# The last four attention steps of a gated cross-attention and FFN layer, ordered in one list with the FFN work that is left

## The chip, the cores and the metric

The kernel runs on one core of a Trainium2 chip. A core has five engines with their own instruction queues: TensorE (PE, matrix products), VectorE (DVE), ScalarE (ACT), GpSimd (POOL) and SyncE (SP, which here issues every DMA). Each runs its own queue strictly in order, and they wait for one another through semaphores. The metric is the time of one execution on the device in microseconds (us); three runs of the kernel before took 3007.0, 3010.42 and 3010.99 us, a median of 3010.42 us.

## The reference

32 batches of 224 tokens (512 wide) attend to 750 context tokens (384 wide) with 16 heads of 32, then go through an FFN of 2048 whose weights are rounded to -1, 0, 1 and whose activations are rounded to 8 bits per token.

```python
def xattn(x, y, pad_mask, Wq, Wkv):          # per batch, 16 heads
    q = x @ Wq.T; k, v = split(y @ Wkv.T)
    attn = softmax(where(mask, q * d**-0.5 @ k.T, -1e9))
    return attn @ v
x = x + tanh(g_xattn) * xattn(layernorm(x), ctx, mask, Wq, Wkv)
x = x + tanh(g_ffn) * ffn(layernorm(x))
# ffn: bitlinear(gelu(bitlinear(x, w1, b1)), w2, b2)
# bitlinear: act_quant(rmsnorm(x)) @ weight_quant(w).T + b
```

## The kernel before

**Attention.** 128 steps (`steps`, N = 128): 32 batches by four groups of four heads, numbered n = 0 to 127. The loop at line 1006, `for n in range(N - 1)`, writes out the work of step n in six slots. The even slots hold one third of the next step's score products for the maxima (`maxima`, line 312: PE writes tile `sm`, DVE reduces it to `mx`); the odd slots hold one third of this step's products, from which ACT takes the exponential (`weights`, line 369: PE writes `se`, ACT writes `p`, POOL adds `p` into `acc`). `sm` and `se` share one buffer of four PSUM banks (`ps_s`), so PE may write the next `sm` only when ACT has read `se`, and the next `se` only when DVE has reduced `sm`. What PE does meanwhile is whatever stands between them in its queue: products for keys (`pk`), values (`pv`), queries (`pq`), the last step's output (`po`, from `p` and `v`), and FFN products. A step opens with `turn_max`: PE turns the negated maxima (`pn`), ACT copies them to `nT`, and `weights` needs `nT`. `finish` and `store` (lines 436 and 445) scale the output on POOL (`yo`) and write it with four DMAs to a DRAM buffer `o_d`.

**FFN.** 28 pairs of 128-row tiles (`NF` = 28, numbers 0 to 27), each cut by `ffn_units` into units: load and fetch (x and `o_d`), add, stats, rsqrt, norm, max, sa0 to sa2 (scales), grid and round (rounding), turn (a transposing DMA); then for each of the two tiles b0 to b3 (four times four products `ph`, DVE writes `h`), gelu and square on ACT, hm (maxima of `h`), sb0 to sb2 (scales, with a chain of small operations for the inverse root), cgrid, cround, cturn (a transposing DMA `hT<-hq`), c0 and c1 (16 products each into `po`, from `w2q` and `hT`) and out. A pair can begin only when the attention rows that it covers are stored; the last pair needs step 127's columns.

**What sets the order.** Engine queues follow program order. In the loop, `Ffn.fill` (line 857) puts FFN units into each slot, as many as `rooms` allow: PE room is 2.5 or 1.9 less what the slot holds, plus `late` (line 888), which is 0.3 for every row tile that is ready but not done beyond a number: `LATE` (3) up to 24 stored batches, and 3 again after that, which is from step 96 on. What is left after step 126 goes to `drain` (line 893): units of the last step (pair number 28 in its list) and of the FFN pairs left, put in order by a planner with a table of durations (`TAKES_US`, line 777); in each turn it takes, of the units that can begin soonest, the one with the longest chain behind it. A unit that can run on either of two engines gets the one that ends it first. There the waits of the last step are listed in `LAST` (line 800), and no gelu may stand before the last exponential, since the two need different ACT tables. Inside the loop each gelu loads its table, and then loads the exponential's again (`b_gelu`, line 671, with the activation `warm`).

Of the kernel before, what the change touches and what calls it, by code (L numbers as in the profile page):

```python
# [24 lines left out]
def flamingo_gated_layer(  # L25
# [495 lines left out]

    draining = []
# [33 lines left out]
    def ffn_units(i):  # L556
# [6 lines left out]
        def a_load():  # L563
            if i >= NF - 2:
                both = yp.tile([P, NYC * M], F32, tag="y", name=f"xo_{i}")
                both = both[:, : 2 * TG * D].rearrange("p (a t d) -> p a t d", a=2, t=TG)
                s["xg"], s["og"] = both[:, 0], both[:, 1]
            else:
# [6 lines left out]
            if i < NF - 1:  # L575
                a_fetch()

        def a_fetch():
            sp.dma_start(s["og"], o_d[rows, :].rearrange("(t p) d -> p t d", p=P))
# [4 lines left out]
        def a_stats():  # L584
            st = smf.tile([P, TG, 6], F32, tag="st2", name=f"st2_{i}")
            s["mv"] = smf.tile([P, TG, 2], F32, tag="mv2", name=f"mv2_{i}")
            for t in range(TG):
                dve.bn_stats(st[:, t, :], s["xg"][:, t, :])
                dve.bn_aggr(s["mv"][:, t, :], st[:, t, :])

        def a_rsqrt():
# [3 lines left out]
            s["nm"] = smf.tile([P, TG], F32, tag="nm2", name=f"nm2_{i}")  # L595
            small[0].tensor_scalar(s["nm"], s["mv"][:, :, 0], -1.0, None, ALU.mult)
# [107 lines left out]
        def c_round(t):  # L704
            if i < NF - 2:
                s["hq", t] = fp.tile([P, F], BF16, tag="hq", name=f"hq_{i}_{t}")
            else:
                s["hq", t] = xp.tile([P, F], BF16, tag="x", name=f"hq_{i}_{t}")
# [24 lines left out]
        if i == NF - 1:  # L733
            first[1:] = [("fetch", 0, "load", 0, 0, 0, a_fetch), ("add", 0, "fetch", 0, 0, 0, a_add)]
# [3 lines left out]
            ("norm", 2, "rsqrt", 0, 1.2, 0, a_norm),  # L738
# [39 lines left out]
        "load": [[("SP", 2.7)]], "fetch": [[("SP", 4.9)]],  # L778
# [12 lines left out]
        "top": [[("PE", 0.3), ("ACT", 0.4)]],  # L791
        "w": [[("PE", 1.1), ("ACT", 1.7)]],
        "val": [[("PE", 2.9), ("DVE", 0.9)]], "vlast": [[("PE", 4.0), ("DVE", 0.9)]],
        "fin": [[("POOL", 0.6)]], "sto": [[("SP", 3.6)]],
    }

    QUEUE_US = {"sto": 1.9, "turn": 1.9, "cturn": 1.5, "load": 0.5, "fetch": 0.5, "out": 0.4}


    LAST = {  # L800
        name: [(NF, at) for at in after.split()]
        for name, after in {
            "w0": "top", "w1": "w0", "w2": "w1", "val": "", "fin0": "val", "sto0": "fin0",
            "vlast": "w2 val", "fin1": "vlast fin0", "sto1": "fin1 sto0",
        }.items()
    }

    class Ffn:
# [3 lines left out]
        def __init__(self):  # L812
# [3 lines left out]
            self.at = {}  # L816

        def behind(self, pair, name):
# [4 lines left out]
                "fetch": [(NF, "sto1")],  # L823
# [4 lines left out]
            if pair >= NF - 2:  # L828
                before = {"fetch": before["fetch"]}
            if name[-1].isdigit():  # L830
# [9 lines left out]
                    f"gelu{t}": [(NF, "w2")] * len(draining),  # L840
# [3 lines left out]
            if pair == NF:  # L844
                before = LAST
            return [at for at in before.get(name, []) if at[0] >= 0]

        def ready(self, pair, unit):
            name, lag, after = unit[:3]
            lag = lag if not draining else 0  # L850
# [37 lines left out]
        def late(self, stored, more):  # L888

            ready = stored * S // P - TG * self.next + sum(p[1][-1][0][:3] == "out" for p in self.parts)  # L890
            return 0.3 * max(0, ready - (LATE if stored < B - 8 else 3) - more)

        def drain(self, more):
# [3 lines left out]
            draining.append(True)  # L897
            free = {"PE": 0.0, "ACT": 0.0, "DVE": 4.3, "POOL": 5.0, "SP": 0.0}
            end = {}

            def takes(name):
                kind = name.rstrip("0123456789")
                return TAKES_US.get(kind) or TAKES_US[kind + name[-1]]

            self.parts.insert(0, [NF, more])
# [3 lines left out]
            left = {}  # L909

            def rank(at):

                if at not in left:
                    left[at] = 0.0
                    left[at] = sum(us for _, us in takes(at[1])[0]) + max(
                        (rank(x) for x in behind if at in behind[x]), default=0.0
# [3 lines left out]
            behind = {  # L920
                (pair, u[0]): [(pair, u[2] or "")] + self.behind(pair, u[0])
                for pair, units in self.parts for u in units
            }

            def course(at, way):

                t = max(
# [198 lines left out]
```

## Time and profile before

| | |
|---|---|
| runs | 3007.0, 3010.42, 3010.99 us; median 3010.42 us |
| the profiled execution | 3009.68 us, of which its span is 3007.9 us |
| busy over the span | PE 2896.7 us (96%), POOL 2087.6 (69%), DVE 1735.9 (58%), ACT 1409.6 (47%) |
| mean granted TensorE clock | 0.989 |
| `pn` of step 96, 124, 127 begins at | 2204.1, 2837.5, 2902.4 us |
| the last store of attention output is issued at | 2929.43 us |

The span runs from the first to the last instruction; 1.8 us lie around it. The rows of `pn` mark where a step begins. A row of the timeline gives start, duration, engine, operation, what it writes and reads, its shape and how many follow one another; in brackets stand the idle time of the engine before it and what ended that. A fp32 product counts as two MATMULs there.

### The profile page before, as it was taken

To read this page: it belongs to the slowest core of one execution; us is meant where nothing else is said; L and a number is where in the kernel's file an instruction comes from. 1 tells how busy PE (TensorE), PEld (TensorE's weight loads), DVE (VectorE), ACT (ScalarE), POOL (GpSimd) and SP (SyncE) were. 2 spreads that over 40 slices of the span, in tenths; PEclk is the share of its full clock that TensorE was granted. 3 is DMA by queue.
4 is the path that set the end of the run, shared out by engine and by line. 5 is a ranking of instruction groups with operands and counts; after the bars stand their busy time and mean duration, and the time that the engine had idled before them with its cause. 6 is when DMAs were issued, how large, how long until landed. Compare 5 with 4: busy or idle time off the path is not lost.

```text
span 3007.9 us, 62728 instructions
## 1 busy us (share of the span) xinstructions
PE 2896.7 (96%) x26790; PEld 1840.5 (61%) x26790; DVE 1735.9 (58%) x2574; ACT 1409.6 (47%) x1401; POOL 2087.6 (69%) x2729
## 2 busy tenths in 40 slices
PE   8999999999999999999999999999999999999976
PEld 4655566566666666666666666666666666666643
DVE  5576565555656555555555556555555655555546
ACT  2344354454545545354454545444544554445444
POOL 3465867768667777776777677766767777677575
PEclk9999999999999999999999999999999999999978
DMA  4343222123222223221222321223122132321123
GB/s 144 92 112 99 54 50 56 49 55 75 60 66 35 67 59 74 68 49 39 66 53 59 71 73 22 76 57 73 47 63 47 47 70 63 75 74 21 38 49 81
DMA packets 352696, 190.02 MB, mean 63 GB/s; under 512 B 282144, under 2 KB 305056, under 8 KB 352288
## 3 DMA queue, kind: packets, MB, share of 16 engines
q1 hardware_dynamic: 352416, 186.01, 25.3%
q8 instruction: 209, 3.42, 0.5%
q14 instruction: 71, 0.58, 0.1%
HBM read 119.86 MB, written 29.39 MB: 50 GB/s over the span
## 4 chain that ended last, share of the span: by engine, by line
PE 80%; ACT 8%; DVE 5%; POOL 3%; DMA 3%; issue 1%; SPq 0%; POOLq 0%; ACTq 0%; DVEq 0%
PE po L52 17%; PE se L52 13%; PE pk L52 13%; PE sm L52 12%; PE pv_None L52 10%; PE ph L52 6%; ACT p L52 5%; PE pq L52 4%; PE pv L52 4%; DVE mx L52 4%; POOL acc L52 2%; ACT L52 1%; ACT h L52 1%; PE pn L52 1%; DMA r_d<-ve 0%
## 5 line engine op out<-in xcount | busy, mean ns | idle before, releaser
L52 POOL TENSOR_TENSOR acc<-acc,p 125x896 f32<-125x896 f32 x510 | 1068.3, 2095 | 300.8 <-ACT p L52 279.5
L52 DVE TENSOR_REDUCE mx<-sm 112x4 f32<-112x2000 f32 (+1 forms) x384 | 861.1, 2242 | 624.3 <-PE sm L52 624.0
L52 ACT ACTIVATE p<-se 125x1792 f32<-125x1792 f32 x384 | 639.1, 1664 | 712.3 <-PE se L52 697.8
L52 PE MATMUL pk<-y,wkv_sb 128*128 128x375 f32 x1536 | 544.8, 491 | 9.7 <-DMA y<-in_ctxT 9.7
L52 PE MATMUL sm<-kT,qT 32*112 32x500 f32 (+1 forms) x4096 | 427.6, 509 | 31.7 <-ACT p L52 22.7
L52 POOL TENSOR_TENSOR acc<-p 125x896 f32<-125x896 f32 x128 | 268.1, 2095 | 244.1 <-ACT p L52 244.1
L52 PEld LDWEIGHTS pk<-y,wkv_sb 128*128 128x128 f32 x1536 | 277.4, 191 | 180.1 <-issue 43.7
L52 PE MATMUL pv_None<-wkv_sb,y 128*125 128x256 f32 x1548 | 367.9, 387 | 0.0
L52 PE MATMUL se<-qT,kT 32*125 32x224 f32 x6144 | 361.1, 350 | 0.0
L52 PEld LDWEIGHTS pv_None<-wkv_sb,y 128*125 128x125 f32 x1548 | 280.2, 187 | 130.6 <-issue 89.8
L52 PE MATMUL po<-p,v 125*32 125x224 f32 x6144 | 320.6, 357 | 0.0
L52 PEld LDWEIGHTS se<-qT,kT 32*125 32x125 f32 x6144 | 296.8, 184 | 0.1
L52 PEld LDWEIGHTS sm<-kT,qT 32*112 32x112 f32 x4096 | 159.6, 171 | 190.0 <-ACT p L52 126.9
L52 ACT COPY kT<-pk 128x375 f32<-128x375 f32 x256 | 120.0, 469 | 309.5 <-PE pk L52 309.0
L52 PEld LDWEIGHTS po<-p,v 125*32 125x32 f32 x6144 | 187.7, 110 | 121.0 <-issue 46.2
L52 DVE SCALAR_TENSOR_TENSOR h<-ph,qa_am,b_sb 128x512 f32<-128x512 f32 x216 | 159.9, 747 | 165.7 <-PE ph L52 143.9
L52 PE MATMUL ph<-w1q,xT 128*128 128x512 fp8e4 x896 | 226.3, 386 | 18.0 <-DMA xT<-xc 15.3
L52 PE MATMUL po<-w2q,hT 128*128 128x256 fp8e4 x1792 | 217.9, 276 | 9.2 <-DMA hT<-hq 9.1
L52 PE MATMUL pq<-xTb,wq_sb 128*128 128x224 f32 x1024 | 220.6, 358 | 1.1 <-DVE wq_sb L52 0.6
L52 PEld LDWEIGHTS pq<-xTb,wq_sb 128*128 128x128 f32 x1024 | 187.3, 190 | 24.5 <-issue 15.5
L52 PEld LDWEIGHTS <-hT 128*128 128x128 bf16 x1792 | 170.2, 99 | 50.7 <-issue 19.4
L52 ACT COPY v<-pv_None 125x512 f32<-125x512 f32 x96 | 56.2, 585 | 308.9 <-PE pv_None L52 308.9
(130 smaller groups left out, 2937.5 us busy)
## 6 DMA issues: line engine op xcount, KB each, us to landing
y<-in_ctxT SPq DMA_DIRECT2D x31, 1125.0 KB, 7.0
x<-in_x SPq DMA_DIRECT2D x32, 448.0 KB, 7.5
xTb<-in_xT SPq DMA_DIRECT2D x32, 448.0 KB, 3.8
o_d<-yo SPq DMA_DIRECT2D x512, 28.0 KB, 1.6
xg<-in_x SPq DMA_DIRECT2D x26, 512.0 KB, 3.7
og<-o_d SPq DMA_DIRECT2D x26, 512.0 KB, 4.6
out<-xg SPq DMA_DIRECT2D x52, 256.0 KB, 2.2
wa<-in_w1T SPq DMA_DIRECT2D x8, 512.0 KB, 7.3
```

The source lines that it names most:

```text
L52: return lambda *args, **kw: tc.keep_in_program_order(build(*args, **kw))
```

## The change

The loop over steps ends at step 123 (`LISTED` = 124). Steps 124 to 127 are cut into units (`last_units`: top, sm0 to sm2, nb, w0 to w2, k0, k1, v0, v1, val, fin, sto; pair numbers 152 to 155 in the list are these four steps) and go into the list of `drain` with pairs 24 (rest) to 27. The planner takes the shared PSUM banks, POOL's additions and a slowed PE into account, and runs 300 times with different weights; the order that its own table calls shortest is written out. Gelu may now stand between the exponentials of these steps, with its two table loads. The last pair fetches its rows of `o_d` in two pieces, 384 columns after step 126's store and 128 columns after step 127's. Buffers of the last two pairs move: pair 26 loads into two `x` buffers, and the rounded `h` of both pairs goes into one `y` buffer. In `late` the number from step 96 on becomes 1 in place of 3. The diff, shortened:

```diff
+    LISTED = N - 4
...
-            if i >= NF - 2:
+            if i == NF - 1:
                 both = yp.tile([P, NYC * M], F32, tag="y", name=f"xo_{i}")
                 both = both[:, : 2 * TG * D].rearrange("p (a t d) -> p a t d", a=2, t=TG)
                 s["xg"], s["og"] = both[:, 0], both[:, 1]
+            elif i == NF - 2:
+                s["xg"] = xp.tile([P, TG, D], F32, tag="x", name=f"xg_{i}")
+                s["og"] = xp.tile([P, TG, D], F32, tag="x", name=f"og_{i}")
             else:
                 s["xg"] = xgp.tile([P, TG, D], F32, tag="xg", name=f"xg_{i}")
                 s["og"] = ogp.tile([P, TG, D], F32, tag="og", name=f"og_{i}")
@@ -573,10 +578,11 @@
                 x.rearrange("b s d -> (b s) d")[rows, :].rearrange("(t p) d -> p t d", p=P),
             )
             if i < NF - 1:
-                a_fetch()
-
-        def a_fetch():
-            sp.dma_start(s["og"], o_d[rows, :].rearrange("(t p) d -> p t d", p=P))
+                sp.dma_start(s["og"], o_d[rows, :].rearrange("(t p) d -> p t d", p=P))
+
+        def a_fetch(cols):
+            of = o_d[rows, cols].rearrange("(t p) d -> p t d", p=P)
+            sp.dma_start(s["og"][:, :, cols], of)
...
+            if i >= NF - 2:
+                minus_mean(dve)
+
+        def minus_mean(engine):
+            s["nm"] = smf.tile([P, TG], F32, tag="nm2", name=f"nm2_{i}")
+            engine.tensor_scalar(s["nm"], s["mv"][:, :, 0], -1.0, None, ALU.mult)
 
         def a_rsqrt():
 
 
             ve = smf.tile([P, TG], F32, tag="ve2", name=f"ve2_{i}")
-            s["nm"] = smf.tile([P, TG], F32, tag="nm2", name=f"nm2_{i}")
-            small[0].tensor_scalar(s["nm"], s["mv"][:, :, 0], -1.0, None, ALU.mult)
...
-                s["hq", t] = xp.tile([P, F], BF16, tag="x", name=f"hq_{i}_{t}")
+                if not home:
+                    home.append(yp.tile([P, TG * F], BF16, tag="y", name="hq_last"))
+                s["hq", t] = home[0][:, t * F : (t + 1) * F]
...
-            first[1:] = [("fetch", 0, "load", 0, 0, 0, a_fetch), ("add", 0, "fetch", 0, 0, 0, a_add)]
+            first[1:] = [
+                ("fetch0", 0, "load", 0, 0, 0, lambda: a_fetch(slice(0, D - P))),
+                ("fetch1", 0, "fetch0", 0, 0, 0, lambda: a_fetch(slice(D - P, D))),
+                ("add", 0, "fetch1", 0, 0, 0, a_add),
+            ]
...
-            ("norm", 2, "rsqrt", 0, 1.2, 0, a_norm),
+            ("norm", 2, "rsqrt" if i < NF - 2 else "stats", 0, 1.2, 0, a_norm),
...
-        "load": [[("SP", 2.7)]], "fetch": [[("SP", 4.9)]],
+        "load": [[("SP", 4.5)]], "fetch0": [[("SP", 4.0)]], "fetch1": [[("SP", 2.8)]],
...
+        "top": [[("PE", 0.3), ("ACT", 0.4)]], "nb": [[("DVE", 1.3)]],
+        "sm": [[("PE", 1.1), ("DVE", 2.3)]],
+        "w0": [[("PE", 1.1), ("ACT", 1.7), ("POOL", 2.1)]],
+        "w1": [[("PE", 1.1), ("ACT", 1.7), ("POOL", 4.2)]],
+        "w2": [[("PE", 1.1), ("ACT", 1.7), ("POOL", 4.2)]],
+        "wlast": [[("PE", 1.1), ("ACT", 1.7)]],
+        "k": [[("PE", 2.0), ("ACT", 0.5)]], "v": [[("PE", 2.8), ("ACT", 0.6)]],
...
+    BANKS = "sm", "w", "wlast"
...
+    def last_units():
+
+        units, after = {}, {}
+
+        def unit(n, name, waits, *do):
+            units.setdefault(n, []).append(
+                (name, 0, None, 0, 0, 0, lambda: [f() for f in do])
+            )
+            after[NF + n, name] = [(NF + m, at) for m, at in waits]
+
+        vs = v_left[:]
+        v_left.clear()
+        for i, at in enumerate(vs):
+            unit(LISTED, f"v{i}", [(LISTED, f"v{i - 1}")][: i], lambda at=at: v_piece(*at))
+        all_v = [(LISTED, f"v{i}") for i in range(len(vs))]
+        kept = {
+            hv: [(LISTED, f"v{i}") for i, at in enumerate(vs) if at[:2] == (B - 1, hv)]
+            for hv in range(2)
+        }
+        for n in range(LISTED, N):
+            at, was = steps[n], steps[n - 1]
+            tail = n == N - 1
+            if n + 2 < N:
+                for i, do in enumerate(k_units(*steps[n + 2])):
+                    unit(n + 2, f"k{i}", [(n + 2, f"k{i - 1}")] * i + [(n - 1, "w2")], do)
+            unit(n, "top", [(n, "nb")], lambda n=n: turn_max(n))
+            for u in range(3):
+                if not tail:
+
+                    unit(
+                        n + 1, f"sm{u}", [(n, f"w{u - 1}") if u else (n - 1, "w2"), (n + 1, "k1")],
+                        lambda n=n, u=u: maxima(*steps[n + 1], u),
+                    )
+                first = [(n + 1, f"sm{u}")] if not tail else [(n, f"w{u - 1}")] * (u > 0)
+                first += [(n, "top")] + [(n - 1, "val")] * (u > 0)
+                unit(
+                    n, f"w{u}" if not tail or u < 2 else "wlast", first,
+                    lambda at=at, u=u: weights(*at, u), *[ended] * (tail and u == 2),
+                )
+            if not tail:
+                unit(n + 1, "nb", [(n + 1, "sm2")], lambda n=n: minus_max(n + 1))
+            for m in (n - 1, n)[: 1 + tail]:
+                on = steps[m]
+                name = "vlast" if m == N - 1 else "val"
+                unit(
+                    m, name,
+                    [(m, "w2" if m < N - 1 else "wlast"), (m - 1, "fin")]
+                    + kept[on[1] // 2] * (on[0] == B - 1),
+                    lambda on=on: values(*on), lambda on=on: sums(*on),
+                )
+                unit(m, "fin", [(m, name), (m - 1, "sto")], lambda on=on: finish(*on))
+                unit(m, "sto", [(m, "fin")], lambda on=on: store(*on))
+        free_y = [(NF + N - 1, "k1")] + [(NF + m, at) for m, at in all_v]
...
+        free_y = [(NF + N - 1, "k1")] + [(NF + m, at) for m, at in all_v]
+        after.update({
+            (NF - 2, "load"): [(NF + LISTED - 1, "sto")],
+            (NF - 1, "load"): [(NF + LISTED - 1, "sto"), (NF - 2, "load")],
+            (NF - 1, "fetch0"): [(NF + N - 2, "sto")], (NF - 1, "fetch1"): [(NF + N - 1, "sto")],
+            (NF - 2, "sa0"): [(NF - 2, "rsqrt")], (NF - 1, "sa0"): [(NF - 1, "rsqrt")],
+            (NF - 2, "cround0"): free_y, (NF - 2, "cround1"): free_y,
+            (NF - 2, "norm"): [(NF + LISTED - 1, "val")] + free_y,
+            (NF - 1, "norm"): [(NF + N - 3, "val")] + free_y,
+            (NF - 2, "turn"): [(NF + N - 3, "w2")] + free_y,
+            (NF - 1, "turn"): [(NF + N - 2, "w2"), (NF - 2, "turn")],
+            (NF - 2, "b10"): free_y,
...
-            lag = lag if not draining else 0
...
-            return 0.3 * max(0, ready - (LATE if stored < B - 8 else 3) - more)
...
+            return 0.3 * max(0, ready - (LATE if stored < B - 8 else 1) - more)
+
+        def drain(self):
+
+
...
+            def course(seed):
+                rng = random.Random(seed)
+                soon = rng.choice((0.6, 1.2, 2.0))
+                vector = rng.choice((0.5, 1.0, 2.0))
+                like = {at: rank(at) + rng.uniform(0.0, 15.0) * (seed > 0) for at in todo}
+                free = {"PE": 0.0, "ACT": 0.0, "DVE": 4.3, "POOL": 5.0, "SP": 0.0}
+                banks, slow, end, order = 3.0, 0.0, {}, []
+                open_ = {at: len(waits[at]) for at in todo}
+                since = {at: 0.0 for at in todo if not open_[at]}
+                while since:
+                    found = []
+                    for at, t in since.items():
+                        t0 = max(t, banks) if kind[at] in BANKS else t
+                        best = None
+                        for way in ways[at]:
+                            if kind[at] == "gelu" and (NF + N - 1, "wlast") not in end:
+                                way = [("ACT", 4.7)]
+                            t, cost = t0, 0.0
+                            for engine, us in way:
+                                t = max(t, free[engine]) + us
+                                cost += vector * us * (engine == "DVE")
+                            if best is None or t + cost < best[0]:
+                                best = t + cost, max(t0, free[way[0][0]]), way
+                        found.append((best[1], -like[at], at, best[2]))
...
+                    last = min(f[0] for f in found) + soon
+                    t, _, at, way = min((f for f in found if f[0] <= last), key=lambda f: f[1])
+                    for i, (engine, us) in enumerate(way):
+                        if engine == "PE":
+                            if t > free["PE"] + 2.0:
+                                slow = t + 3.2
+                            us += min(us, max(0.0, slow - t) / 2)
+                        t = max(t, free[engine])
+                        free[engine] = t + (QUEUE_US[kind[at]] if engine == "SP" else us)
...
+            us, _, order = min(course(seed) for seed in range(300))
+            for at, way in order:
                 small[0] = {"DVE": dve, "POOL": gp}.get(way[-1][0], act)
...
-    for n in range(N - 1):
+    for n in range(LISTED):
...
-    last = steps[-2:]
-    ffn.drain(
...
+    ffn.drain()
```

## The prediction

> **What bounds the kernel now.** I read the page's slices of the granted TensorE clock first, then the busy time by stage, with the stages cut where `pn` opens steps 96, 124 and 127. The columns are length, then busy us (and count) of PE, PEld, DVE, ACT, POOL, the granted clock, the DMA share, GB/s.
>
> ```profile
> PEclk9999999999999999999999999999999999999978
> ```
>
> ```profile
> 2204.10:2837.50 633.40, 627.99 (x5864) 399.68 (x5860) 366.61 (x546) 307.65 (x307) 455.43 (x593) 1.00 0.24 57
> 2837.50:2902.40 64.90, 51.71 (x538) 31.30 (x534) 37.85 (x55) 31.13 (x31) 45.83 (x61) 0.90 0.14 35
> 2902.40:3007.90 105.50, 69.64 (x513) 43.02 (x510) 58.04 (x96) 46.56 (x33) 61.96 (x133) 0.80 0.33 73
> ```
>
> Up to step 124 PE is the bound: 628.0 of 633.4 us busy, clock 1.00, 5.4 us idle in 28 steps. From there it is latency: steps 124 to 126 leave PE idle 13.2 of 64.9 us, and the last stretch 35.9 of 105.5, at clocks of 0.90 and 0.80. So the change has something to win in the last 170.4 us, and before that it can only lose or move work.
>
> Next the timeline of PE and ACT, for what an empty slot costs.
>
> ```profile
> 2289.40 0.93 PE L52 MATMUL se<-qT,kT 32*125 32x224 f32 x16
> 2290.26 1.78 PE L52 MATMUL pq<-xTb,wq_sb 128*128 128x224 f32 x8
> 2292.20 1.11 PE L52 MATMUL sm<-kT,qT 32*112 32x500 f32 x8 [0.16 <-ACT p L52]
> ...
> 2766.68 1.11 PE L52 MATMUL sm<-kT,qT 32*112 32x500 f32 x8 [0.37 <-ACT p L52]
> ...
> 2833.16 0.93 PE L52 MATMUL se<-qT,kT 32*125 32x224 f32 x16
> 2834.02 1.04 PE L52 MATMUL ph<-w1q,xT 128*128 128x512 fp8e4 x4
> 2834.89 1.68 PE L52 MATMUL pq<-xTb,wq_sb 128*128 128x224 f32 x8
> 2836.50 1.11 PE L52 MATMUL sm<-kT,qT 32*112 32x500 f32 x8
> ...
> 2840.93 0.41 PE L52 MATMUL se<-nT,ones 3*125 3x448 bf16 x4 [1.17 <-ACT nT L52]
> ...
> 2883.99 0.64 PE L52 MATMUL se<-nT,ones 3*125 3x448 bf16 x4 [2.16 <-DVE mx L52]
> 2884.42 1.70 PE L52 MATMUL se<-qT,kT 32*125 32x224 f32 x16
> ```
>
> ```profile
> 2835.93 1.28 ACT L52 ACT_TABLE_LOAD   x1
> 2837.22 1.91 ACT L52 ACTIVATE h<-h 128x2048 f32<-128x2048 f32 x1
> 2839.15 1.28 ACT L52 ACT_TABLE_LOAD   x1
> 2840.56 0.33 ACT L52 COPY nT<-pn 128x224 bf16<-128x224 bf16 x1
> ```
>
> With `pq` alone between `se` and the next `sm`, `se` to `sm` takes 2292.20 - 2289.40 = 2.80 us. With four `ph` in front of the same `pq` it takes 3.34, of which `ph` is 0.87 (2834.89 - 2834.02). So without FFN work the slot wastes 2.80 - (3.34 - 0.87) = 0.33 us. A half `pv` alone wastes 0.37 (the bracket). If a gelu with its two table loads stands on ACT ahead of `nT`, and PE has only `pk` to run, it waits 1.17. And in 2884.42 `se` takes 1.70 in place of 0.93: half clock, after idle times of about 2 us.
>
> Last, the chain that ended last, its final pieces (start, length, what).
>
> ```profile
> 2994.42 2.01 ACT hq L52
> ...
> 2996.45 4.26 DMA hT<-hq
> ...
> 3000.75 3.68 PE po L52 x32
> ...
> 3004.46 0.48 DVE xo L52
> ```
>
> A tile's end is rounding on ACT (2.0), transpose (4.3), 32 products (3.7), DVE (0.5): waiting, not throughput.
>
> **The change, part by part.** All against the profiled execution (span 3007.9, time 3009.68; the median of the runs is 0.7 above that). Orders are those in which the two built programs list their instructions on each engine.
>
> *Steps 96 to 123.* The number in `late` falls from 3 to 1, which gives each slot up to 0.6 more room, so `fill` takes FFN units as soon as they are ready and later slots find none. In the lists the slots with `pq` alone go from 10 to 21, with half a `pv` alone from 7 to 11, with `pk` alone between `pn` and `se` from 6 to 10; in three of these four more a gelu stands directly ahead of `nT` on ACT. Cost: 11 x 0.33 = 3.6; 4 x 0.37 = 1.5; 3 x 1.17 = 3.5; the fourth 0.2 (another such row, 2295.68, waits 0.21 for DVE). Idle: 8.8. Moved across the border are 12 `ph` (2.6 us, 0.216 each) out of the end and one `sm` group (1.04) into it: 1.6. Sum **+10.4**. Bounds: +1.6 if the slots cost nothing, +14 if each costs half as much again.
>
> *Steps 124 to 126.* I laid the list's instructions on their engines in its order with the durations of these rows. PE work is 55.5 us: three `po` 2.78, nine `sm` 1.04, four `pk` 2.0, nine `se` 1.11, two `pv` 2.8, eight `ph` groups 0.86, four `c` groups 1.75, `pn` 0.3. Two new waits stand in step 124. (a) `val` of step 123 comes straight after `top`, and its sums need `acc`, for which POOL adds 4.2 us after step 123's last `p`: PE waits 2.1, and `sm0` and all else on PE behind it. The table has no such wait for that unit. (b) Ahead of `sm1`'s reduction DVE has a `v` copy 0.7, pair 25's grid 2.3 and round 1.75, and pair 24's scales, ten small operations at 0.2 (the pitch of the 128x2 ones at 2952; DVE has not run this chain before; on POOL it takes 3.3, and 3.3 is the upper bound, 1.6 the lower). PE has one `pv` to run meanwhile and then idles 5.2, with `w1`, pair 25's `ph` and `sm2` queued behind. The rest is the known alternation, seven waits of 0.5 to 2.5 for `mx` (6.7 in all), four for `p` (3.0), and 2.9 at half clock. 55.5 + 2.1 + 5.2 + 6.7 + 3.0 + 2.9 = 75.4, against 64.9: **+10.5** (0 if the extra 8.9 us of FFN work all fall into idle time that is there now; +14 with the upper bound for (b)).
>
> *From `pn` of step 127 to the last store's first DMA*: now 27.0, by the list 26.1: **-0.9**. Pair 26's `ph` and two tiles of pair 25 lie in it.
>
> *From there to the end*: now 2929.43 to 3007.9, 78.5. By the list the chain is: stores landed 2.9, 128 columns landed 3.9 (rows of 3.9 and 5.1 for 512 columns; below, 1.6 as the stores take), add on POOL 2.4, pair 26's cgrid 2.0, cround 2.0, transpose 4.3; 32 products after a long wait 5.2, DVE 0.5, scales 1.0, cgrid 2.0, cround 2.0, transpose 4.3; 32 products 3.7, DVE 0.5, two maxima and scales 2.9, cgrid 1.3, cround 2.0, transpose 4.3; 64 products 9.4, DVE 0.5, out 2.2; 14 steps of issue at 0.05. Sum 60.0: **-18.5**. Two tiles of pair 25 are now done before the store, and pair 26 is at its rounding when pair 27 begins; that is the gain.
>
> *At nothing*: moved buffers (pair 26 loads while step 124 runs, and no unit of the chain above waits for it; uncovered, a load is 3.7 to 4.7 us), `minus_mean` on DVE (0.2, in DVE's idle time; uncovered, 0.4), the first 384 columns (issued behind step 126's store; late, they would stand in front of pair 25's transpose on SP for 0.4).
>
> *What such a sum leaves out.* Laying before's own last 105.5 us this way gives 103: landings of 2.9 in place of 1.6 behind transposes, cold starts. I add **+2.5**, and **+2.1** for cold starts of the products after the three transposes (0 to 4).
>
> Sum: 10.4 + 10.5 - 0.9 - 18.5 + 2.5 + 2.1 = **+6.1**, so 3010.4 + 6.1 = **3016.5 us**.
>
> Two rules of the Trainium skill read differently. "TensorE: Matmul & The Clock Gate", "Why this matters for your kernels", puts the fall to half clock at idle gaps above about 3 us. The row at 2883.99 shows it after 2.16, so the row counts; by the page the 2.9 us at half clock in steps 124 to 126 would shrink to some 1.5, and the sum to 3015. "ScalarE: Activation LUTs", "What ACT_TABLE_LOAD costs", gives 2.66 us for a switch with its drain, and "Table sets" says to do all of one set before switching, which speaks against gelus among the exponentials. Here the load is 1.28 and the next instruction starts 1.29 later; by the page the three gelus ahead of `nT` would cost 3 x 2 x 1.38 = 8.3 us more, and the sum would be 3024.8.
>
> **The rivals.** *The emptied slots cost nothing*: FFN work done earlier is not done later, and ACT's lead hides the rest. For it: 28 steps now lose only 5.4 us, with 17 such slots among them. Against: each such slot has its idle time in the rows. Then 3016.5 - 8.8 = 3007.7, no change; this is the case that is not slower, and it decides if `pn` of step 124 comes within 4 us of 2837.5. *Step 124 does not stall*: if `acc` is done before `val` and DVE has passed pair 25's work before `sm1` is written, 2.1 + 5.2 go: 3009.2. For it: POOL and DVE are 69% and 58% busy; against: both are in-order lists with the work in front. Only both rivals together (3000.4) make it faster. *SP holds up the end*: the 128 columns wait behind pair 25's transposes, and a late hq holds SP in front of the fetch (it held SP from 2962.5 to 2968.9 now): +6.4 for one such wait, 3022.9; it decides if the fetch is issued over 6 us after the last store.
>
> **Chances.** The forecast 0.60, with a range of its own from 3010 to 3022, six tenths of it beyond 0.2%; emptied slots free 0.13; no stall 0.10; both together 0.07; SP 0.10. A measurement can tell 0.2%, 6.0 us, from no change. Slower by more: 0.36 + 0.10 = 0.46; faster: 0.07 and 0.04 from the lower bounds of the single rivals = 0.11; within: 0.43, the rest. The range 3007 to 3024 leaves out 3000.4 and the far ends of the bounds.
>
> **What would show it.** `pn` of step 124 near 2848 and PE idle near 15 us in steps 96 to 123; a wait of PE of about 5 us for DVE in step 124 and of 2 for POOL; step 127 opening near 2923; the last store near 2949, and 60 to 65 us after it. It is wrong if step 124 begins by 2841, or if less than 55 or more than 68 us follow the last store.

## The result, and the profile after

The changed kernel takes 3019.63 us (median of 8 runs, 3015.17 to 3023.14); the kernel before, on the same chip, 3010.83 (8 runs, 3007.0 to 3013.73). The ratio is 1.0027, with a 95% interval from 1.0017 to 1.0038: slower by a quarter of a per cent. The profiled execution took 3015.17 us (span 3013.4), the shortest of the eight.

The stages of the changed kernel's span, columns as in the prediction (length, then busy us and count of PE, PEld, DVE, ACT, POOL, granted clock, DMA share, GB/s):

```profile
2203.70:2848.70 645.00, 631.48 (x5868) 401.03 (x5865) 374.00 (x558) 318.38 (x316) 461.00 (x621) 1.00 0.24 57
2848.70:2926.10 77.40, 61.78 (x595) 36.42 (x593) 49.49 (x86) 35.01 (x34) 45.56 (x40) 0.93 0.17 43
2926.10:3013.40 87.30, 55.81 (x446) 35.26 (x446) 44.18 (x101) 37.88 (x27) 44.56 (x75) 0.80 0.31 69
```

Steps 96 to 123 take 11.6 us more, steps 124 to 126 take 12.5 more, and what follows 18.2 less; up to step 96 it is 0.4 less. Together +5.5 us of span. PE's idle time in steps 96 to 123 has grown from 5.4 to 13.5 us. PE's waits there show where (who waits for whom: us in total, times, longest):

```profile
PE se L53 <- ACT nT L53: 5.6, 4, 1.7
PE sm L53 <- ACT p L53: 4.4, 13, 0.4
PE se L53 <- DVE mx L53: 1.2, 6, 0.2
```

Before, the same three were 0.3, 2.6 and 1.2 us. One of the four waits for `nT`, in PE's and ACT's timeline:

```profile
2343.81 2.12 PE L53 MATMUL pk<-y,wkv_sb 128*128 128x375 f32 x6
2347.63 0.41 PE L53 MATMUL se<-nT,ones 3*125 3x448 bf16 x4 [1.70 <-ACT nT L53]
2347.82 0.98 PE L53 MATMUL se<-qT,kT 32*125 32x224 f32 x16
2348.73 2.16 PE L53 MATMUL pk<-y,wkv_sb 128*128 128x375 f32 x6
```

```profile
2342.62 1.28 ACT L53 ACT_TABLE_LOAD   x1
2343.92 1.91 ACT L53 ACTIVATE h<-h 128x2048 f32<-128x2048 f32 x1
2345.85 1.28 ACT L53 ACT_TABLE_LOAD   x1
2347.14 0.20 ACT L53 ACTIVATE warm<-magic 128x1 f32<-128x1 f32 x1
2347.25 0.33 ACT L53 COPY nT<-pn 128x224 bf16<-128x224 bf16 x1
```

The gelu of pair 19 stands ahead of `nT` with both table loads, and PE has one `pk` group of 2.1 us for 4.5 us of ACT.

In steps 124 to 126 the two largest idle times of PE are these (the bracket gives the idle time and what ended it):

```profile
2853.43 0.59 PE L53 MATMUL po<-acc,ones 125*32 125x224 f32 x8 [2.06 <-POOL acc L53]
2854.99 5.74 PE L53 MATMUL pk<-y,wkv_sb 128*128 128x375 f32 x12
2873.73 0.64 PE L53 MATMUL se<-nT,ones 3*125 3x448 bf16 x4 [5.29 <-DVE mx L53]
```

Twelve `pk` products took 5.74 us, where the same twelve took 4.05 at full clock in e3: here the first idle time is followed by half clock. (In four kernels below the same idle time is not; the last section shows why.) For the second, DVE's timeline shows what stood ahead of the maximum:

```profile
2864.65 0.69 DVE L53 COPY v<-pv_None 125x512 f32<-125x512 f32 x1 [5.02 <-PE pv_None L53]
2865.26 3.24 DVE L53 TENSOR_SCALAR xc<-xc,qa_c 128x512 f32<-128x512 f32 x2
2868.53 0.69 DVE L53 TENSOR_SCALAR xq<-xc 128x1024 bf16<-128x1024 f32 x1
...
2871.44 2.23 DVE L53 TENSOR_REDUCE mx<-sm 112x8 f32<-112x2000 f32 x1
```

Beside the two grid instructions (`xc<-xc,qa_c`) POOL was adding:

```profile
2863.65 2.08 POOL L53 TENSOR_TENSOR acc<-p 125x896 f32<-125x896 f32 x1 [7.96 <-ACT p L53]
2865.68 2.54 POOL L53 TENSOR_TENSOR xg<-xg,og 128x1024 f32<-128x1024 f32 x1
```

The last pieces of the chain that ended last, the rounding and transpose of pair 27's second tile and the products of both, are of the same kinds as before; there are now two `po` rows, since two tiles end together, the first at half clock (6.33 for 3.68):

```profile
2995.55 4.24 DMA hT<-hq_last
2999.84 6.33 PE po L53 x32
3006.18 3.68 PE po L53 x32
```

### The profile page after: what moved, and what is told of

Its sections match the earlier page's. It is cut to its first block, busy times and chain, and to the rows that moved or that the text cites. A ratio compares the mean times of both kernels' runs of the same rounds, so it can differ in the third digit from the quotient of the medians.

```text
span 3013.4 us, 62742 instructions
## 1 busy us (share of the span) xinstructions
PE 2896.7 (96%) x26790; PEld 1839.7 (61%) x26790; DVE 1741.3 (58%) x2623; ACT 1414.8 (47%) x1407; POOL 2072.6 (69%) x2679
## 4 chain that ended last, share of the span: by engine, by line
PE 78%; ACT 9%; POOL 5%; DVE 4%; DMA 3%; issue 1%; SPq 0%; ACTq 0%; POOLq 0%; DVEq 0%
PE po L53 17%; PE se L53 13%; PE pk L53 12%; PE sm L53 12%; PE pv_None L53 11%; ACT p L53 6%; PE ph L53 6%; DVE mx L53 4%; PE pv L53 3%; PE pq L53 3%; POOL acc L53 2%; ACT L53 1%; ACT h L53 1%; POOL r_a L53 1%; POOL h L53 1%
## 5 line engine op out<-in xcount | busy, mean ns | idle before, releaser
L53 PE MATMUL po<-w2q,hT 128*128 128x256 fp8e4 x1792 | 220.5, 278 | 25.8 <-DMA hT<-hq_last 17.7
L53 POOL TENSOR_TENSOR yo<-oT,rd 128x224 f32<-128x224 f32 x128 | 75.7, 592 | 186.9 <-DVE rd L53 128.8
```

Source lines behind the costliest of these rows:

```text
L53: return lambda *args, **kw: tc.keep_in_program_order(build(*args, **kw))
```

## The experiments

All were run in turn with the kernel before. The stages are those of one profiled execution each (us): "to last store" is from `pn` of step 127 to the issue of the last store's first DMA, "to end" from there to the end of the span, and "tail" is from `pn` of step 124 to the end. The ratio is to before, with its 95% interval. The first 96 steps, the same code in all, took 2202.6 to 2208.2 us, so I compare stages, and medians beside them.

| kernel | steps 96-123 | 124-126 | to last store | to end | tail | median us | ratio |
|---|---|---|---|---|---|---|---|
| before | 633.4 | 64.9 | 27.0 | 78.5 | 170.4 | 3010.83 | 1 |
| changed | 645.0 | 77.4 | 25.7 | 61.6 | 164.7 | 3019.63 | 1.0027 (1.0017-1.0038) |
| e1 before, late 1 | 648.0 | 62.3 | 27.7 | 78.4 | 168.4 | 3026.09 | 1.0048 (1.0035-1.006) |
| e2 changed, late 3 | 632.3 | 77.0 | 24.0 | 69.4 | 170.4 | 3010.3 | 0.9997 (0.9989-1.0006) |
| e3 val later | 645.0 | 71.0 | 25.0 | 62.4 | 158.4 | 3014.01 | 1.001 (1.0001-1.0019) |
| e4 late 3, other table | 632.3 | 67.0 | 23.4 | 72.0 | 162.4 | 3005.14 | 0.9979 (0.997-0.9988) |
| e5 grid behind the maximum | 646.7 | 71.1 | 25.8 | 61.8 | 158.7 | 3013.91 | 1.0006 (0.9998-1.0015) |
| e6 one fetch | 645.0 | 77.1 | 25.1 | 62.5 | 164.7 | 3017.7 | 1.0022 (1.0013-1.0031) |
| e7 first order | 646.6 | 78.2 | 28.2 | 68.0 | 174.4 | 3028.84 | 1.0054 (1.0042-1.0067) |
| e8 gelu behind nT | 647.3 | 77.4 | 26.2 | 62.2 | 165.8 | 3020.9 | 1.0034 (1.0023-1.0045) |
| e9 e3 and e5 | 645.0 | 70.1 | 25.5 | 63.6 | 159.2 | 3012.8 | 1.0006 (0.9997-1.0015) |
| e10 late 1, other table | 645.0 | 81.2 | 23.8 | 60.1 | 165.1 | 3020.06 | 1.0024 (1.0015-1.0034) |
| e11 late 4, other table | 624.7 | 70.3 | 25.5 | 86.1 | 181.9 | 3011.77 | 1.0002 (0.9993-1.0011) |
| e12 addition later | 646.7 | 74.1 | 25.7 | 62.2 | 162.0 | 3016.15 | 1.0016 (1.0007-1.0025) |

### e1 and e2: the late number and the list, each alone

e1 is the kernel before with

```diff
-            return 0.3 * max(0, ready - (LATE if stored < B - 8 else 3) - more)
+            return 0.3 * max(0, ready - (LATE if stored < B - 8 else 1) - more)
```

> The kernel before with one edit: the late number of the last eight steps is 1 in place of 3; its list of steps 124 to 127 is as it was. My theory (the prediction's): the number draws ready work into earlier slots and leaves later slots of steps 96 to 123 without work, so these steps take 642 to 648 us in place of 633.4, and little of it comes back: the tail from step 124 to the end, which has less work left, is shorter by 0 to 3 us. Time about 8 us above before (3016 to 3022), ratio 1.002 to 1.0035. Rival (emptied slots are free, since the work done early is missing later): steps 96 to 123 may grow, but the tail shrinks by as much, and the time lies within 2 us of before.

The stages came as expected: 648.0, and a tail only 2.0 us shorter. PE's waits in steps 96 to 123 are the changed kernel's to the digit:

```profile
PE se L52 <- ACT nT L52: 5.6, 4, 1.7
PE sm L52 <- ACT p L52: 4.4, 13, 0.4
PE se L52 <- DVE mx L52: 1.2, 6, 0.2
```

The time went beyond my range: 3026.09, ratio 1.0048. Of the profiled execution's extra 16.7 us of span, 12.6 are these two stages (14.6 - 2.0) and 4.1 lie before step 96, where the code is unchanged: chance, and 3.4 of it two pieces at half clock more, as 1.7 of the 648.0 is one (told of below). The rival is out: of the 14.6 us that the work done early cost, 2.0 came back.

e2 is the changed kernel with the same line set back to 3.

> The changed kernel with one edit back: the late number is 3 again; the four steps are still units of the list and the columns are still fetched by themselves. More work is left for the list, which orders itself anew. My theory: steps 96 to 123 take 632 to 635 us again, steps 124 to 127 some 75 to 78 (with a wait for VectorE's maximum or its like inside), from the pn of step 127 to the last store 22 to 24, and from there to the end 69 to 72; time 3006 to 3012, ratio 0.9985 to 1.0003. Rival (the list's own waits are the loss, and the number's share is small): 3015 to 3020, with steps 96 to 123 not much shorter than 645 or the tail longer by what they gain.

As expected: steps 96 to 123 are back at 632.3, and the time is before's (0.9997). So without the number in `late` nothing of the change's loss is left. The list with late at 3 has a tail of 170.4 us, exactly before's: its 12.1 us more in steps 124 to 126 and its 12.1 less behind them cancel. In the list the early work is paid back in part: the tail is 164.7 us with late at 1, 5.7 shorter, for 12.7 more in steps 96 to 123.

### e8: is it the gelu's place in ACT's queue?

Four gelus are issued one place later, behind `nT`:

```diff
+            if held := getattr(self, "held", None):
+                self.held = held()
...
-                unit[6]()
+                if (pair, unit[0]) in ((18, "gelu1"), (19, "gelu1"), (23, "gelu0"), (23, "gelu1")):
+                    self.held = unit[6]
+                else:
+                    unit[6]()
```

> The changed kernel, with four gelu activations in steps 98 to 119 issued one place later: they stood directly ahead of nT on ScalarE (se waited for nT 1.7, 1.7, 0.5 and 1.7 us there), and now stand directly behind it, in the same slot, with the same work beside them. My theory: the loss is that a gelu with its two table loads (4.5 us of ScalarE) stands in a slot that has too little TensorE work left, not which neighbour it delays; so the waits for nT go, but the kT copy and the exponential behind the gelu are late instead, steps 96 to 123 take 644 to 648.5 us (645.0 in the changed kernel), and the time stays within 2 us or is up to 3 us longer. Rival (the place in ScalarE's queue is the cause, as the prediction puts it): these 5.6 us come back, steps 96 to 123 take 639 to 641, ratio 1.001.

Steps 96 to 123 took 647.3 us, as my theory had it; the rival, which was the prediction's own wording, would have had 640. PE's waits in this stage:

```profile
PE sm L53 <- ACT p L53: 11.2, 18, 1.7
PE se L53 <- DVE mx L53: 2.1, 10, 0.2
```

No wait for `nT` is left, and 6.8 us more of waits for the exponentials `p` have come. The gelu with its loads delays whatever stands behind it, by what the slot's PE work lacks.

### e3, e5, e9 and e12: the two stalls of step 124

Each edit reorders the finished list; only the pairs (unit, unit to stand behind) differ.

```diff
             us, _, order = min(course(seed) for seed in range(300))
+            for x, y in (
+                ((NF + 123, "val"), (NF + 124, "w0")),
+                ((NF + 123, "fin"), (NF + 123, "val")),
+                ((NF + 123, "sto"), (NF + 123, "fin")),
+            ):
+                names = [at for at, _ in order]
+                move = order.pop(names.index(x))
+                names.remove(x)
+                order.insert(names.index(y) + 1, move)
```

> The changed kernel, with three units of its list moved by hand: the output projection val of step 123, its fin and its store go behind w0 of step 124, nothing else. The stall this is about: po waits 2.06 us for GpSimd's acc at 2853.4. My theory: the wait falls to 0.3 us or less, and 1.5 to 3 us of the time go with it (ratio to before about 1.002). Rival: acc's lateness is not on the path, because the next wait (se for mx, 5.3 us) grows by what this one loses: no change from the changed kernel (1.0027).

Steps 124 to 126 fell by 6.4 us, the median by 5.6, more than the 1.5 to 3 expected. The wait for `acc` is gone, and the second stall has shrunk too:

```profile
2849.10 4.05 PE L53 MATMUL pk<-y,wkv_sb 128*128 128x375 f32 x12
...
2866.55 0.41 PE L53 MATMUL se<-nT,ones 3*125 3x448 bf16 x4 [2.91 <-DVE mx L53]
```

2.06 is the wait, 2.38 the other wait (5.29 - 2.91), and 1.69 the `pk` row, 4.05 for 5.74. This last part is not the edit's: behind a wait of 2.04 to 2.06 us for `acc` the twelve `pk` took 4.05 in e5, e7, e8 and e12 too, which leave `val` where it was. That the second wait shrinks was not foreseen. In this kernel DVE's two grid instructions took 0.48 us each (3.24 in all in the changed kernel); nothing ran on POOL beside them. In the changed kernel POOL's addition for pair 26 did, from 2865.68 to 2868.22.

e5 takes pair 25's grid, round and turn and pair 24's sb10 out of the reduction's way: grid behind sm1 of step 125, the other three behind it in a row.

> The changed kernel, with four units of its list moved by hand on VectorE and SP: grid, round and turn of pair 25 and sb10 of pair 24 go behind sm1 of step 125, so that the reduction mx of that step no longer stands behind them; nothing else. The stall this is about: se waits 5.29 us for mx at 2873.7. My theory: the order on VectorE's queue is the cause of the stall, so the wait at that place falls to 1 to 2.5 us (what is left is the v copy ahead and the reduction's own 2.2), but the moved units feed pair 25, which is then late by as much: from step 124 to the last store 1 to 3 us are gained, and 0 to 3 at the end; ratio to before 1.0015 to 1.0027. Rival (the reduction is late because its sm or the v copy is late, not for what stands ahead of it): the wait stays at 4 us or more.

The stall of 5.29 us vanished, and my theory's second half was wrong: it was not given back. Steps 124 to 126 shrank by 6.3 us, and the time with them (ratio 1.0006 for 1.0027); only a wait of 2.48 us of `ph` for pair 25's `xT` took its place. Here too the grid, which now begins 0.14 us before the addition's end, took 0.88. The wait for `acc` is still there, and this time no half clock follows it:

```profile
2859.65 0.58 PE L53 MATMUL po<-acc,ones 125*32 125x224 f32 x8 [2.05 <-POOL acc L53]
...
2861.20 4.05 PE L53 MATMUL pk<-y,wkv_sb 128*128 128x375 f32 x12
```

e9 does both.

> The changed kernel (late at 1) with both moves by hand at once: val, fin and store of step 123 behind w0 of step 124, and grid, round, turn of pair 25 and sb10 of pair 24 behind sm1 of step 125. Each alone took 5 to 6 us from the changed kernel's time. My theory: they are two stalls with two causes, so the gains add in the main: steps 124 to 127 take 65 to 68 us (77.4 in the changed kernel), ratio to before 0.9985 to 0.9998, the time about that of before, with late still at 1. Rival (they share one thing, the half clock that the first gap leaves behind, so that the second move has little left to gain): steps 124 to 127 take 70 us or more, ratio 1.0003 to 1.001.

My theory fell: 70.1 us, hardly less than with either alone, ratio 1.0006. The rival's figures came, but not its reason: the half clock behind the first gap is gone in e5 as well, where the gap stands. What the two moves share is the meeting with POOL's addition, which either undoes. The 2.91 us that e3 leaves at the second place are traded, when the grid moves too, for 2.70 us of `ph` waiting for `xT`. And what e9 wins over e5 at the first place, the 2.05 us for `acc`, it mostly loses at the second: eight `ph` products ran at half clock behind the 2.70 us (3.41), and at full clock behind e5's 2.48 (1.90).

e12 leaves DVE's units up to the maximum where they were and moves POOL's addition out from beside the grid:

```diff
+                ((NF - 2, "add"), (NF + 124, "w1")),
+                ((NF - 2, "stats"), (NF + 125, "nb")),
```

> The changed kernel, with two units of pair 26 moved by hand: its addition xg<-xg,og on GpSimd goes behind w1 of step 124, its stats on VectorE behind nb of step 125. VectorE's own units up to the late maximum of step 125 keep their order. In the changed kernel this addition (2865.68 to 2868.22) ran beside VectorE's grid of pair 25, whose two pieces took 0.75 and 2.57 us; in the two kernels with moved units, where no such addition ran beside it, a piece took 0.48. My theory: the grid stood still until the addition was over, and that is 2.3 us of the 5.29 us wait of se for mx: now both pieces take 0.48, the wait falls to 2.5 to 3.3 us, steps 124 to 127 take 72.5 to 75.5 (77.4), the wait of 2.06 for acc stays; ratio 1.0008 to 1.0022. Rival (the grid was slow for a reason of its own, or the wait is set by something else in front of the reduction): the grid stays above 2 us, or the wait stays at 5; ratio 1.0027.

```profile
2864.16 1.14 DVE L53 TENSOR_SCALAR xc<-xc,qa_c 128x512 f32<-128x512 f32 x2
...
2870.52 0.64 PE L53 MATMUL se<-nT,ones 3*125 3x448 bf16 x4 [3.18 <-DVE mx L53]
```

The grid took 1.14 in place of 3.24 (its start still met the end of POOL's addition to `acc`), the wait 3.18 in place of 5.29, the stage 74.1, the ratio 1.0016: as expected but for the first piece of the grid. So 2.1 of the 5.29 us are DVE standing still beside POOL, shown by this run; the rest is the queue. Of the stage's 3.3 us some 1.7 are something else, which the edit does not touch: the `pk` behind the wait for `acc` took 4.05 for 5.74.

### e6: the fetch of the last columns by themselves

```diff
-                ("fetch0", 0, "load", 0, 0, 0, lambda: a_fetch(slice(0, D - P))),
-                ("fetch1", 0, "fetch0", 0, 0, 0, lambda: a_fetch(slice(D - P, D))),
+                ("fetch0", 0, "load", 0, 0, 0, lambda: None),
+                ("fetch1", 0, "fetch0", 0, 0, 0, lambda: a_fetch(slice(0, D))),
```

> The changed kernel, with the whole of the last pair's input fetched at once behind the last store (fetch1 takes all columns, fetch0 nothing); the list's order is the same. My theory: in the changed kernel the chain that ended last does not run through this fetch (it runs through hT of pair 26), so the larger fetch lands later without being waited for: time as the changed kernel's within 1.5 us, ratio 1.002 to 1.0032. Rival (fetching the last columns by themselves is what shortens the end): 2 to 4 us more than the changed kernel, ratio 1.0035 to 1.0045, and xo stands in the chain.

As expected: 3017.7 us, and an interval that overlaps the changed kernel's nearly whole. POOL's addition for pair 27, which waits for the fetch, began 8.3 us after the last store in place of 6.7, and the transpose `hT` issued just behind the 512 KB took 6.66 us in place of 4.26; yet the end came only 0.9 us later. In this list the split is worth about that at most.

### e7, e10, e11 and e4: which order, and how much work it gets

e7 writes out the order of seed 0 in place of the shortest of 300.

> The changed kernel with the first of its 300 orders in place of the one its planner holds for shortest; by the planner's own table this order takes 152.3 us in place of 148.45. My theory: the table misses the stalls that cost most (acc on GpSimd, VectorE's grid and round), so its ranking is only rough: the end comes 1 to 3 us later than in the changed kernel, with less time from step 127 to the last store (some 22 for 25.7) and more from there to the end (66 for 61.6); ratio 1.003 to 1.004. Rival (the table ranks rightly, the choice among 300 is what the list is worth): 4 us or more later, ratio 1.004 or above; or it ranks not at all, and this order is as fast as the chosen one or faster.

The first rival's figure came: ratio 1.0054, a tail of 174.4 us, 9.7 more than the chosen order, where the planner's own values differ by 3.85. I had put too little on the choice. That the table ranks rightly does not follow; see e10.

e4 has late at 3 and other entries for the planner:

```diff
-        "norm": [[("ACT", 1.4)], [("DVE", 1.0)]], "max": [[("DVE", 1.2)]],
+        "norm": [[("ACT", 1.4)], [("DVE", 1.9)]], "max": [[("DVE", 1.2)]],
...
-        "sa2": [[("DVE", 0.5)], [("POOL", 0.8)]], "grid": [[("DVE", 1.0)], [("POOL", 1.4)]],
-        "bias": [[("POOL", 2.5)], [("DVE", 1.3)]], "round": [[("ACT", 1.2)], [("DVE", 0.9)]],
+        "sa2": [[("DVE", 0.5)], [("POOL", 0.8)]], "grid": [[("DVE", 2.4)], [("POOL", 1.4)]],
+        "bias": [[("POOL", 2.5)], [("DVE", 1.3)]], "round": [[("ACT", 1.2)], [("DVE", 1.8)]],
...
-        "cround": [[("ACT", 2.0)], [("DVE", 1.8)]], "cturn": [[("SP", 3.8)]],
+        "cround": [[("ACT", 2.0)], [("DVE", 1.8)]], "cturn": [[("SP", 4.3)]],
...
-                since = {at: 0.0 for at in todo if not open_[at]}
+                since = {at: 5.0 * (at == (NF + LISTED - 1, "val")) for at in todo if not open_[at]}
```

> The changed kernel with late at 3, and with a planner that is told what the trace shows: val of step 123 can't begin in the first 5 us of the list, and in its table of durations grid on VectorE is 2.4 (was 1.0), round 1.8 (0.9), norm 1.9 (1.0) and the turn of the last pairs 4.3 (3.8). It chooses among 300 orders as before. My theory: steps 96 to 123 take 633 us, 124 to 127 some 67 to 70 because neither po nor se waits more than a microsecond or so, then 22 to 24 and 70 to 73; time 2999 to 3006, ratio 0.996 to 0.9985, so faster than both. Rival (what the list gains inside the steps it gives back at the end, where less work is left for the cover): 3008 to 3013.

The figures held, and it beats both kernels: 3005.14 us, ratio 0.9979. The reason given did not: no wait of `po` for `acc` is left in steps 124 to 126, but `se` still waits for `mx`, 9.4 us in six waits (10.9 in seven in the changed kernel):

```profile
PE se L53 <- DVE mx L53: 9.4, 6, 3.0
```

Its stages (compare 77.0 and 93.4 in e2):

```profile
2839.80:2906.80 67.00, 54.04 (x544) 30.52 (x543) 48.30 (x79) 35.10 (x35) 41.28 (x52) 0.92 0.17 42
2906.80:3002.20 95.40, 63.66 (x510) 40.42 (x510) 56.16 (x105) 50.14 (x38) 52.42 (x103) 0.84 0.33 75
```

e10 gives the same table to the list with late at 1.

> The changed kernel (late at 1) with the mended planner alone: val of step 123 not before 5.0 us, grid 2.4, round 1.8 and norm 1.9 on VectorE, turn of the last pairs 4.3; the order is chosen anew among 300. With late at 3 the same planner gave 0.9979. My theory: the planner and the late number pay apart from each other: steps 96 to 123 take 645 to 648 us as in the changed kernel, and from step 124 to the end 155 to 160 (164.7 there), ratio 1.0005 to 1.0015. Rival (the planner was all, and late is worth nothing once the list has no stalls, since the work done early is then missing in the list): 0.998 to 0.9985.

Neither was right: ratio 1.0024, a tail of 165.1, no better than the changed kernel's 164.7, with one wait of 5.1 us for `mx` again. So the entries do not make better orders as such; e4's gain is that of one good order. Grid at 2.4 was in fact the length beside POOL; in e4 the two grids that ran on DVE in the tail took 0.87 and 3.08. The planner's own values for the tail were 148.45 (changed), 152.3 (e7), 151.95 (e10), 161.95 (e2), 162.2 (e4) and 168.7 (e11), where 164.7, 174.4, 165.1, 170.4, 162.4 and 181.9 were measured: short by 16.2, 22.1, 13.1, 8.4, 0.2 and 13.2. A value that can be off by so much can't tell orders apart that lie within a few us of one another.

e11 leaves still more for the list.

> The changed kernel with the mended planner and late at 4, so that still more FFN work is left for the list than at 3. My theory: there is a best point, since work moved out of steps 96 to 123 frees TensorE only until no slot there is overfull, and what comes behind the last attention step lies bare behind transfers and table loads: steps 96 to 123 take 622 to 626 us (632.3 at 3), from step 124 to the end 172 to 178 (162.4 at 3), ratio 0.999 to 1.0003, no better than at 3. Rival (the fewer units stand in steps 96 to 123, the better): steps as said, the end within 5 us of 162.4, ratio 0.996 to 0.9975.

624.7 us in steps 96 to 123, but a tail of 181.9, more than I expected; the time is before's. 7.6 us less there, 19.5 more behind it: with the same table, 3 is better than 4 and than 1.

## Why the prediction was right, and where it was off

The time forecast was 3016.5, and 3019.63 came, inside the range. Against the profiled execution the sum was +6.1 and +5.5 came; the medians lie 8.8 apart because the profiled execution happened to be the shortest of its eight. So the closeness to 5.5 is in part luck: against the medians the sum is 2.7 short, and no trace shows where the longer executions spend it.

*Steps 96 to 123.* +10.4 by the sum, +11.6 measured, `pn` of step 124 at 2848.7 (2848 foretold). e1 shows that the number alone does this. By terms: idle 8.1 (13.5 - 5.4) for 8.8, PE's busy time +3.5 for +1.6, which the rows do not take apart. Inside the idle time the parts were mis-sized in opposite ways. The waits for `nT` cost 5.3 more, where three at 1.17 and a fourth at 0.2 made 3.7: three were 1.70, as ACT was free only after both loads. Slots with `pq` or half a `pv` alone cost less than the 5.1 priced: the waits for `p` grew by 1.8, the rest of the idle time by 1.0. The words "directly ahead of `nT`" named a symptom: e8 moved the four gelus behind `nT` and lost 2.3 us more.

*Steps 124 to 126.* +10.5 foretold, +12.5 measured. The two waits came as described, 2.06 for 2.1 and 5.29 for 5.2, the other waits for `mx` were 5.6 for 6.7, those for `p` 2.5 for 3.0. Two terms were mis-sized, PE's work and the half clock: PE was busy 61.8 us where the sum had 55.5 of work and 2.9 at half clock. By the rows, against the same rows at full clock in e5, the half clock cost 4.4: 1.7 in `pk` behind the first wait, 1.1 in `se` and 1.6 in `ph` behind the second. That leaves some 57.4 for the work, 1.9 more than the sum had (an estimate; e9, with a granted clock of 0.98, has 59.0 of busy time in all). The 1.7 came by chance, as e5 shows. The 5.2 was right by luck in its parts: grid 3.24 for 2.3, round 0.69 for 1.75. Both prices came from rows in which I had not seen what POOL did beside them: the kernel before rounds from 2922.75 for 1.76 us, while POOL adds from 2922.68 to 2925.63. In this way the price of an operation on DVE was taken for its own when it was partly POOL's.

*The end.* To the last store 25.7 for 26.1, from there 61.6 for 60.0 and the 4.6 us of allowances: the allowances were too large by 3.0.

*The rivals.* "The emptied slots cost nothing" fell with e1, "step 124 does not stall" with the two rows. "SP holds up the end" did not occur: the fetch was issued at 2955.71, 4.0 us after the last store where 6 was the point, and e6 shows room behind it for a transfer four times as large.

*The rules weighed.* For the clock, "TensorE: Matmul & The Clock Gate" of the Trainium skill would have made the term 1.5 in place of 2.9; the trace has 4.4, and the rows of the last section show half clock after 1.70, so the measurement decides against 3 us as the least gap. For the table loads, each was 1.28 and the next instruction began 1.29 to 1.30 after its start, with no drain between; the sum by "ScalarE: Activation LUTs" (3024.8) lies above all eight runs.

Open: why e4's order is so good (its waits for `mx` are hardly shorter), and how e1's time came to 14.4 us over before where its stages explain 12.6 (the other runs of e1 were not profiled).

## What to carry to other kernels

Where the bound engine is busy without a gap, filler work that is drawn forward may shorten what comes later by little: here by 2.0 us of the 14.6 that it cost (e1), or 5.7 of 12.7 (the changed kernel against e2). For the rest it empties slots in which another engine's long step then lies bare. Price such a filler by the slot it leaves empty, not by its own time. A stall near the end costs its wait and sometimes the half clock behind it, 2.06 us and 1.7 more in one row here, 2.05 and nothing more in another; look first for a unit that can change places with the one that waits. And before a planner's best of 300 is taken, hold its value against a trace: here it was short by 0.2 to 22 us.

## What was not expected of the hardware

A grid instruction of DVE stands still while POOL adds. It (128x512, fp32 from and to SBUF) takes 0.48 us alone; in the changed kernel its two took 0.75 and 2.57, the second ending 0.28 us after POOL's addition of 128x1024. e12, which moves that addition away, shows it, and e3 agrees. Not every DVE instruction does: in e5 the reduction `mx`, which reads PSUM, ran beside the same addition and took its usual 2.24 us.

```profile
2870.20 2.34 POOL L53 TENSOR_TENSOR xg<-xg,og 128x1024 f32<-128x1024 f32 x1
2870.24 2.24 DVE L53 TENSOR_REDUCE mx<-sm 112x8 f32<-112x2000 f32 x1 [0.38 <-PE sm L53]
```

"SBUF — State Buffer" of the Trainium skill, "SBUF: two separate sides", says this of the port pair that the two engines share: for the kinds of DVE instruction that it lists, whichever of the two starts first has the pair for its whole instruction, and the other blocks. The rows agree; the profile does not name the port.

TensorE's clock falls in pieces of 3.41 us, and one idle time of 1.70 us can be enough. The `pk` behind the wait for `nT` shown above takes 2.16 us in the changed kernel; in e5, after the same wait, it takes 3.85 at a granted clock of 0.50 (the second fence is the window over it):

```profile
2352.18 0.41 PE L53 MATMUL se<-nT,ones 3*125 3x448 bf16 x4 [1.70 <-ACT nT L53]
2352.36 0.98 PE L53 MATMUL se<-qT,kT 32*125 32x224 f32 x16
2353.27 3.85 PE L53 MATMUL pk<-y,wkv_sb 128*128 128x375 f32 x6
```

```profile
2353.50:2356.90 3.40, 3.40 (x6) 1.43 (x5) 0.00 (x0) 3.40 (x3) 2.66 (x11) 0.50 0.01 2
```

The same code and wait, 1.7 us apart. In each of the 14 traces the half clock begins and ends on one grid of 3.41 us, and these rows go by how much of an idle time falls into one piece of that grid. Two pieces around the wait for `acc` of step 124, first in the changed kernel, then in e5 (after the length stands PE's busy time):

```profile
2851.72:2855.13 3.41, 1.70 (x17) 0.59 (x18) 0.86 (x3) 0.59 (x1) 1.67 (x2) 1.00 0.02 5
2855.13:2858.54 3.41, 3.41 (x6) 1.92 (x7) 3.38 (x3) 0.00 (x0) 0.56 (x1) 0.50 0.23 34
```

```profile
2855.30:2858.70 3.40, 2.30 (x48) 1.30 (x40) 0.23 (x1) 3.24 (x5) 3.29 (x2) 1.00 0.05 7
2858.70:2862.10 3.40, 2.45 (x19) 1.09 (x20) 1.61 (x3) 0.00 (x0) 1.46 (x2) 1.00 0.02 5
```

With PE idle for half of one piece (1.71 us) the next ran at half clock; with the same wait cut in two by the border (1.10 and 0.95) it did not. The other four kernels with this wait agree: half clock in e6 (2.05 us idle in one piece), none in e7, e8 and e12 (at most 1.41, 1.47 and 1.03). Half a piece is near the edge: two other waits of 1.70 us in e5, which also lie whole in one piece (from 2254.5 and from 2742.6), were followed by full clock. The four kernels with 646.6 us or more in steps 96 to 123 that are not e8 (e1, e5, e7, e12) have a piece at half clock there, and the first 96 steps, one code, have from two (e3, e12) to five (e1, e4, e5). So some of the scatter between executions of one kernel is of this kind.
